# Layers 0 and 1 of a four-layer graph network: smaller parts of the orders' work, queued on VectorE behind the eviction of the sums they follow

## The chip, the cores and the metric

The kernel runs on one core of a Trainium2 chip, in fp32. The metric is the device time of one launch in microseconds (us), lower is better. TensorE does the matmuls and transposes, VectorE (DVE in the profile), ScalarE (ACT) and GpSimd (POOL) the elementwise work, SyncE (SP) issues most of the loads. [...] engines wait for each other at semaphores.

## The reference

Sixteen graphs of 1024 nodes with 256 features run through four layers, each of the form x = x + f(relu(layernorm(x)), adj). Layers 0 and 1 are one pass over the adjacency each; layer 2 updates the nodes one after the other, each from those before it; layer 3 is a sum and two dense layers.

```python
# layer 0
u = mask * jnp.exp(logits)                     # logits = e[:, :, None] + f[:, None, :] + a_b
a = u / jnp.sum(u, axis=2, keepdims=True)
h_prime = jnp.einsum('bnm,bmd->bnd', a, h)
# layer 1
d_inv_sqrt = (jnp.sum(adj, axis=-1) + 1e-05) ** (-0.5)
adj_norm = d_inv_sqrt[..., :, None] * adj * d_inv_sqrt[..., None, :]
return jnp.einsum('bnm,bmo->bno', adj_norm, support) + bias
# layer 2: a scan over i = 0 .. n-1
x_par = jnp.einsum('bj,bjd->bd', row, h)       # row = norm_adjT[:, i]
iou = x @ W_ioux.T + b_ioux + x_par @ W_iouh.T + b_iouh
h_new = z * x_par + (1.0 - z) * hc
# layer 3
neighbor_sum = jnp.einsum('bnm,bmd->bnd', adjacency, x)
h = jax.nn.silu(_rmsnorm(h, rms_weight))
```

## The kernel before

Layers 0 and 1 are one function, `layers_0_1`; layers 2 and 3 follow, and the change doesn't touch them. Batches run in a software pipeline: iteration i does layer 0 of batch i and layer 1 of batch i-1.

`layer_0(b)` first multiplies the adjacency with the exponentials `gs` (L361, into `pd`), then makes the neighbour sums in four groups of eight 128x512 matmuls (L309, `sums`). There are two groups for each half of the nodes: ScalarE evicts the first of a half (L312), VectorE the second (L314). Then come the row sums (L371), the reciprocals (L373 to L375), and the dense product (L379), which VectorE adds to x (L380). `layer_1(b)` does the same sums from `h1`, a product (L410) with its eviction (L411), the statistics, and `h2` (L301). The sums have two PSUM buffers (`pa`), the products two (`pmm`).

Between the four groups of a sum the lists `between` and `slots` put other jobs: `reshape` (statistics and h1 for layer 1), `prepare(i + 1)` (statistics, `q` at L340, `f` at L342, the exponential `gs` at L347 on ScalarE, the scaling at L352) and, from iteration 9 on, `put_in_order` for two batches (one in the last two iterations). `put_in_order` puts blocks of the adjacency and of h2 in layer 2's order: it loads `ad` (L423, L424) and `ab` (L427), masks and scales `ad` on GpSimd (L435 to L440), builds the permutation `to` (L432), transposes on TensorE (L448, L461, L463), evicts by turns on ScalarE and VectorE (L450, L452, L468, L470), multiplies (L476, L482), and writes `heT_d`, `near_d`, `next_d` and `base_d` through GpSimd's queue (L454, L472, L473, L485).

The orders are layer 2's plan, made from the zeros of the diagonal blocks. `places()` is a greedy pass over 128 positions: five small VectorE operations for each (L135 to L140), with the adjacency loaded in eight pieces of 16 (`piece`, L113, into a tile named `ad`). Then 8 pairs of 128x2048 operations rank the positions (L149, L151), and a transpose gives `place`, which `put_in_order` needs. `rest()` inverts the order with 128 operations (L162), writes the tables for the gathers of layer 2 (L174 to L181), makes a chain pass with eight pieces again (L195, L196), and counts the extra rounds (L201 to L236). Both are generators: `slot` takes the next part of `places` in each of the four slots of an iteration, from the start; `between[1]` and `between[3]` take one of `rest` from iteration 9 (`ready`) on.

The queue of each engine isn't this program order. A scheduler walks the program with a priority in the order of the text, puts an instruction into its engine's queue as soon as, by its own estimates, the inputs and a free buffer are there, and so may move work that is ready past work that still waits. Nothing in the kernel before ties the orders to a place in VectorE's queue. The pool `big01` has one buffer of most names; `ad` is one, shared by the pieces of both passes, the 128x2048 tiles of the ranking and `put_in_order`.

Of the kernel before, what the change touches and what calls it, by code (L numbers as in the profile page):

```python
# [9 lines left out]
F32 = mybir.dt.float32  # L10
# [30 lines left out]
def gnn_stack(ctx: ExitStack, tc: tile.TileContext, a: dict, out: bass.AP):  # L41
# [65 lines left out]
    def orders(pool, psum):  # L107
# [18 lines left out]
        def places():  # L126
            nc.vector.memset(bins, TOP)
            nc.vector.tensor_scalar(open_, step[:, :S], -1.0, TOP - 1, op0=ALU.mult, op1=ALU.add)
            nc.vector.tensor_scalar(below, open_, 1.0, None, op0=ALU.add)
            nc.vector.memset(held, 0.0)  # L130
            for j0 in range(0, P, S):
                nz = piece(j0, ALU.is_equal, 2 * TOP)
                for j in range(j0, j0 + S):
                    mine = bins[:, j : j + 1]
                    nc.vector.scalar_tensor_tensor(fit, below, mine, open_, op0=ALU.is_le, op1=ALU.mult)  # L135
                    nc.vector.tensor_reduce(mine, fit, AX.X, ALU.max)
                    nc.vector.scalar_tensor_tensor(held, open_, mine, held, op0=ALU.is_equal, op1=ALU.add)
                    nc.vector.scalar_tensor_tensor(open_, held, float(S), open_, op0=ALU.is_lt, op1=ALU.mult)
                    if j + 1 < P:
                        nc.vector.scalar_tensor_tensor(bins[:, j + 1 :], nz[:, j - j0, j + 1 :], mine, bins[:, j + 1 :],  # L140
                                                       op0=ALU.add, op1=ALU.min)
                    if j % 8 == 7:
                        yield

            key = tile_("key")
            nc.vector.scalar_tensor_tensor(key, bins, -256.0, step, op0=ALU.mult, op1=ALU.add)
            for i in range(0, P, S):
                less = pool.tile([P, S, P], F32, name="ad")
                nc.vector.tensor_tensor(less, key[:, None].to_broadcast([P, S, P]),  # L149
                                        key[:, i : i + S][:, :, None].to_broadcast([P, S, P]), ALU.is_lt)  # L150
                nc.vector.tensor_reduce(pos[:, i : i + S], less, AX.X, ALU.add)  # L151
                yield
            pt = psum.tile([P, 512], F32, name="pt")
            nc.tensor.transpose(pt[:, :P], pos, ident)
            nc.vector.tensor_copy(place, pt[:, :P])
            yield

        def rest():

            node = tile_("key")  # L160
            for p in range(P):
                nc.vector.scalar_tensor_tensor(junk, pos, float(p), step, op0=ALU.is_equal, op1=ALU.mult,  # L162
                                               accum_out=node[:, p : p + 1])
                if p % 32 == 31:
                    yield
# [17 lines left out]
            yield  # L183

            sub = tile_("sub")
            nc.vector.memset(sub, 0.0)
# [4 lines left out]
            for j0 in range(0, P, S):  # L191
                nz = piece(j0, ALU.not_equal, 2.0)
                for j in range(j0, min(j0 + S, P - 1)):
# [3 lines left out]
                                                   op0=ALU.mult, op1=ALU.max)  # L197
                yield
            top = tile_("top", NS)
            for s in range(NS):  # L200
                nc.vector.scalar_tensor_tensor(junk, sub, float(s), chain, op0=ALU.is_equal, op1=ALU.mult)  # L201
                nc.vector.tensor_reduce(top[:, s : s + 1], junk, AX.X, ALU.max)
# [34 lines left out]
            yield  # L237
        return places(), rest()

# [7 lines left out]
    def layers_0_1():  # L247
        with ExitStack() as st:
# [46 lines left out]
            def normed(x, scale, mv, name, bufs):  # L295
# [6 lines left out]
                return h  # L302

            def sums(at, h, ag):

                def part(n0, c):
# [6 lines left out]
                    else:  # L313
                        nc.vector.tensor_copy(ag[:, c, n0 : n0 + 512], pa)  # L314
                return [lambda n0=n0, c=c: part(n0, c) for n0 in (0, 512) for c in range(DC)]
# [39 lines left out]
            def layer_0(b, between):  # L355
# [9 lines left out]
                for part in sums(at[b], q[b], ag):  # L365
                    part()
                    if between:
                        between.pop(0)()
# [32 lines left out]
            def layer_1(b, between):  # L401
                ag = big.tile([P, DC, N], F32, name="ag", bufs=2)
                for part in sums(at[b], h1[b], ag):
                    part()
                    if between:
                        between.pop(0)()
# [85 lines left out]
            when.update({b + 2: (b,) for b in range(14, B)})  # L492
            parts_of_places, parts_of_rest = orders(big, psum)
            load(0)
# [3 lines left out]
            for i in range(B + 2):  # L498
                if i + 1 < B:
                    load(i + 1)  # L500
                jobs = []
                for b in when.get(i, ()):
# [12 lines left out]
                def slot():  # L515
                    for part in slots.pop(0):
                        part()
                    next(parts_of_places, None)
                if i < B:
# [6 lines left out]
                if 0 < i < B - 1:  # L526
# [3 lines left out]
                    between[1] = lambda: (load_half(i + 1), second())  # L530
                if i >= ready:
                    between += [lambda: None] * (4 - len(between))
                    for k in (1, 3):
                        between[k] = lambda part=between[k]: (part(), next(parts_of_rest, None))
                if 1 <= i <= B:
# [734 lines left out]
```

## Time and profile before

| | us |
|---|---|
| median of 3 runs | 4856.29 (4855.62 to 4856.56) |
| the profiled execution | 4861.04 |
| its span | 4858.2 |
| TensorE busy | 4494.9 |
| VectorE busy | 2303.1 |
| GpSimd busy | 1586.6 |
| ScalarE busy | 1220.2 |
| layers 0 and 1: first matmul of layer 2 | 1507.7 |

The profile is of one execution. Durations of one instruction are means of it unless a start is named; a group of one line can count records, not instructions (an fp32 matmul leaves two). "Idle before, releaser" tells what ended the idle time of an engine. A share of busy time is an average over stages with different limits, so the stage of layers 0 and 1, the first 31% of the span, has to be read by itself.

### The profile page before, as it was taken

To read this page: it belongs to the slowest core of one execution; us is meant where nothing else is said; L and a number is where in the kernel's file an instruction comes from. 1 tells how busy PE (TensorE), PEld (TensorE's weight loads), DVE (VectorE), ACT (ScalarE), POOL (GpSimd) and SP (SyncE) were. 2 spreads that over 40 slices of the span, in tenths; PEclk is the share of its full clock that TensorE was granted. 3 is DMA by queue.
4 is the path that set the end of the run, shared out by engine and by line. 5 is a ranking of instruction groups with operands and counts; after the bars stand their busy time and mean duration, and the time that the engine had idled before them with its cause. 6 is when DMAs were issued, how large, how long until landed. Compare 5 with 4: busy or idle time off the path is not lost. (4 is left out here: it accounts for less than half of the span.)

```text
span 4858.2 us, 52472 instructions
## 1 busy us (share of the span) xinstructions
PE 4494.9 (93%) x18199; PEld 3004.6 (62%) x18199; DVE 2303.1 (47%) x6354; ACT 1220.2 (25%) x2629; POOL 1586.6 (33%) x1939
## 2 busy tenths in 40 slices
PE   8998899999997999999999999998899999999999
PEld 4443455555555777777777777776455555555556
DVE  6667854455543444444444444454534344344342
ACT  1211112222212222222322222222223223223232
POOL 3223233343323322332232323331534234243231
PEclk9999999999998999999999999998899999999999
DMA  4333235555537444444344544420422231222100
GB/s 157 113 99 104 88 88 183 194 165 176 184 104 209 149 137 133 149 142 149 115 140 122 157 139 153 142 82 29 169 87 70 78 104 65 91 88 78 70 26 18
DMA packets 530978, 576.61 MB, mean 119 GB/s; under 512 B 42544, under 2 KB 439472, under 8 KB 528304
## 3 DMA queue, kind: packets, MB, share of 16 engines
q1 hardware_dynamic: 499536, 460.27, 30.6%
q0 software_dynamic: 31040, 111.44, 6.4%
q8 instruction: 197, 3.23, 0.3%
q14 instruction: 205, 1.68, 0.1%
HBM read 469.65 MB, written 116.65 MB: 121 GB/s over the span
## 5 line engine op out<-in xcount | busy, mean ns | idle before, releaser
L309 PE MATMUL pa<-at,h 128*128 128x512 f32 x1088 | 497.4, 610 | 32.9 <-DVE ag L314 32.9
L1145 PE MATMUL ph<-ag,w 128*128 128x512 f32 x1024 | 478.3, 609 | 32.7 <-DVE hh L1149 32.4
L1183 PE MATMUL po<-w,hh 128*128 128x256 f32 x2048 | 447.7, 379 | 0.0
L637 PE MATMUL pf<-hb,ab 128*128 128x256 f32 x1568 | 420.6, 387 | 29.0 <-DVE bxt L787 16.2
L1183 PEld LDWEIGHTS po<-w,hh 128*128 128x128 f32 x2048 | 387.8, 190 | 59.3 <-issue 7.9
L309 PE MATMUL pa<-at,q 128*128 128x512 f32 x960 | 424.2, 595 | 0.0
L309 PEld LDWEIGHTS pa<-at,h 128*128 128x128 f32 x1088 | 209.9, 196 | 278.5 <-issue 232.8
L749 PE MATMUL pf<-hs,wx 128*128 128x256 f32 x1536 | 351.1, 383 | 16.6 <-POOL hs L740 14.9
L1145 PEld LDWEIGHTS ph<-ag,w 128*128 128x128 f32 x1024 | 178.6, 189 | 294.0 <-DVE hh L1149 151.4
L1151 POOL TENSOR_TENSOR ss<-ss,sq 128x512 f32<-128x512 f32 x224 | 304.9, 1361 | 118.7 <-ACT sq L1148 114.3
L749 PEld LDWEIGHTS pf<-hs,wx 128*128 128x128 f32 x1536 | 292.1, 192 | 60.1 <-POOL hs L740 16.8
L637 PEld LDWEIGHTS pf<-hb,ab 128*128 128x128 f32 x1568 | 278.2, 192 | 69.5 <-DVE bxt L787 23.4
L309 PEld LDWEIGHTS pa<-at,q 128*128 128x128 f32 x960 | 178.2, 190 | 216.1 <-issue 212.6
L1149 DVE TENSOR_SCALAR hh<-ph,b 128x512 f32<-128x512 f32 x256 | 189.8, 746 | 153.8 <-ACT sq L1148 120.5
L784 PE MATMUL pf<-bd,h 128*128 128x384 f32 (+5 forms) x768 | 214.4, 373 | 51.7 <-DVE bxt L787 26.5
L1034 POOL DMA_INDIRECT hs_d<-h,table x128 | 129.3, 1010 | 365.4 <-ACT gates L757 179.7
L1130 PE MATMUL pa<-bxt,h 128*128 128x512 f32 x512 | 227.9, 597 | 18.6 <-POOL bxt L1112 18.6
L1130 PE MATMUL pa<-at,h 128*128 128x512 f32 x512 | 228.8, 597 | 0.0
L1148 ACT ACTIVATE sq<-ph,b 128x512 f32<-128x512 f32 x224 | 153.6, 686 | 233.6 <-PE ph L1145 188.2
L787 DVE TENSOR_TENSOR bxt<-bxt,pf 128x384 f32<-128x384 f32 (+5 forms) x384 | 141.2, 384 | 149.1 <-PE pf L784 146.6
L1175 ACT ACTIVATE hh<-hh,rw 128x512 f32<-128x512 f32 x256 | 168.4, 712 | 138.5 <-DVE hh L1174 136.5
L754 DVE TENSOR_TENSOR gates<-pf,bias 128x512 f32<-128x512 f32 x128 | 88.4, 691 | 227.3 <-PE pf L749 227.3
(253 smaller groups left out, 7318.6 us busy)
## 6 DMA issues: line engine op xcount, KB each, us to landing
at<-in_adjT SPq DMA_DIRECT2D x64, 1024.0 KB, 7.2
ab<-in_adj SPq DMA_DIRECT2D x128, 512.0 KB, 4.0
bxt<-in_adjT SPq DMA_DIRECT2D x64, 512.0 KB, 5.8
at<-in_adjT SPq DMA_DIRECT2D x64, 512.0 KB, 5.8
ad<-in_adj SPq DMA_DIRECT2D x128, 128.0 KB, 6.0
x_d<-x POOLq DMA_DIRECT2D x16, 1024.0 KB, 5.4
he_d<-h POOLq DMA_DIRECT2D x16, 1024.0 KB, 9.5
heT_d<-hT POOLq DMA_DIRECT2D x16, 1024.0 KB, 4.4
```

Of the source, the lines that this page charges most:

```text
L309: nc.tensor.matmul(pa, h[:, mt, c * P : (c + 1) * P], at[n0 // 512][:, mt], start=mt == 0, stop=mt == NT - 1)
L637: nc.tensor.matmul(pb, ab[:, jts[k]], hb[:, jts[k]], start=k == 0, stop=k == len(jts) - 1)
L749: nc.tensor.matmul(pg[:, e], wx[:, c, q * D + e * P : q * D + (e + 1) * P], self.hs[:, c], start=c == 0, stop=c == DC - 1)
L784: nc.tensor.matmul(pf, h[:, g, c * P : (c + 1) * P], bd[:, g, b4 : b4 + 4, S : S + far], start=True, stop=True)
L787: return lambda: nc.vector.tensor_add(to, to, pf)
L1130: nc.tensor.matmul(pa, h[b][:, mt, c * P : (c + 1) * P], at[b][n0 // NH][:, mt], start=mt == 0, stop=mt == NT - 1)
L1145: nc.tensor.matmul(ph, w1[:, c, k * P : (k + 1) * P], ag[:, c, n0 : n0 + NH], start=c == 0, stop=c == DC - 1)
L1148: nc.scalar.activation(sq, ph, AF.Square, bias=b1[:, k : k + 1])
L1149: nc.vector.tensor_scalar(hh[:, k], ph, b1[:, k : k + 1], None, op0=ALU.add)
L1151: nc.gpsimd.tensor_tensor(ss, ss, sq, ALU.add)
L1175: nc.scalar.activation(hh[:, k], hh[:, k], AF.Silu, scale=rw[:, k : k + 1])
L1183: nc.tensor.matmul(po, hh[:, c, k * P : (k + 1) * P], w2[:, c], start=c == 0, stop=c == HC - 1)
```

## The change

The orders' generators are cut into smaller parts, in three instead of two, and moved. A part of `places` is three positions instead of eight, or eight rows of the ranking instead of sixteen (the tile is half as large); a part of the new `tables` is eight of the L162 instead of 32; the chain pass, in the new `rounds`, yields after every eighth position instead of every sixteenth. The scratch `junk` of `rounds` is a tile of the name `ad` now.

`sums` keeps VectorE's evictions in the list `taken`, and `some_of(parts)` runs one part under `tc.issue_after(taken[-1].ins)`: each instruction that the part puts on VectorE's queue stands behind that eviction there. Instructions on other engines, its loads among them, aren't tied. `some_of` follows each of the four groups of a sum: in layer 0 with `places` before batch 9 and `tables` from there, in layer 1 with `places` and from batch 8 on `rounds`. What is left of `places` at iteration 9 runs at its start. The earlier calls in `slot` and `between` are gone.

```diff
-                    if j % 8 == 7:
+                    if j % 3 == 2:
                         yield
 
             key = tile_("key")
             nc.vector.scalar_tensor_tensor(key, bins, -256.0, step, op0=ALU.mult, op1=ALU.add)
-            for i in range(0, P, S):
-                less = pool.tile([P, S, P], F32, name="ad")
-                nc.vector.tensor_tensor(less, key[:, None].to_broadcast([P, S, P]),
-                                        key[:, i : i + S][:, :, None].to_broadcast([P, S, P]), ALU.is_lt)
-                nc.vector.tensor_reduce(pos[:, i : i + S], less, AX.X, ALU.add)
+            yield
+            for i in range(0, P, 8):
+                less = pool.tile([P, 8, P], F32, name="ad")
+                nc.vector.tensor_tensor(less, key[:, None].to_broadcast([P, 8, P]),
+                                        key[:, i : i + 8][:, :, None].to_broadcast([P, 8, P]), ALU.is_lt)
+                nc.vector.tensor_reduce(pos[:, i : i + 8], less, AX.X, ALU.add)
                 yield
...
-        def rest():
+        def tables():
...
-                if p % 32 == 31:
+                if p % 8 == 7:
                     yield
...
             yield
 
+        def rounds():
+
             sub = tile_("sub")
...
-                yield
+                    if j % 8 == 7:
+                        yield
             top = tile_("top", NS)
+            junk = pool.tile([P, P], F32, name="ad")
...
-        return places(), rest()
+        return places(), tables(), rounds()
...
+            taken = []
+
+            def some_of(parts):
+
+                with tc.issue_after(taken[-1].ins):
+                    next(parts, None)
+
             def sums(at, h, ag):
...
-                        nc.vector.tensor_copy(ag[:, c, n0 : n0 + 512], pa)
+                        taken.append(nc.vector.tensor_copy(ag[:, c, n0 : n0 + 512], pa))
...
                 for part in sums(at[b], q[b], ag):
                     part()
+                    if taken:
+                        some_of(places if b < ready else tables)
                     if between:
                         between.pop(0)()
...
                 for part in sums(at[b], h1[b], ag):
                     part()
+                    some_of(places if b + 1 < ready else rounds)
                     if between:
                         between.pop(0)()
...
+                if i == ready:
+                    for _ in places:
+                        pass
...
                     for part in slots.pop(0):
                         part()
-                    next(parts_of_places, None)
...
-                if i >= ready:
-                    between += [lambda: None] * (4 - len(between))
-                    for k in (1, 3):
-                        between[k] = lambda part=between[k]: (part(), next(parts_of_rest, None))
```

More of the change, by code (lines that the diff above doesn't have):

```diff
@@ L492, in layers_0_1 @@
             when.update({b + 2: (b,) for b in range(14, B)})
-            parts_of_places, parts_of_rest = orders(big, psum)
+            places, tables, rounds = orders(big, psum)
             load(0)
```

## The prediction

> **What bounds the kernel now.** I read the page first, then the clock and busy times stage by stage, then who TensorE waited for in the stage that the change touches, then the timelines of TensorE and VectorE around the longest wait.
>
> ```profile
> PE 4494.9 (93%) x18199; PEld 3004.6 (62%) x18199; DVE 2303.1 (47%) x6354; ACT 1220.2 (25%) x2629; POOL 1586.6 (33%) x1939
> ...
> 120.00:735.00 615.00, 556.03 (x1707) 281.82 (x1706) 417.88 (x1614) 108.50 (x227) 172.26 (x163) 0.96 0.33 98
> 735.00:1443.00 708.00, 673.08 (x2461) 382.34 (x2460) 360.51 (x1088) 143.65 (x288) 257.36 (x274) 0.98 0.53 173
> 1443.00:1508.00 65.00, 36.42 (x147) 26.50 (x146) 28.15 (x117) 9.57 (x18) 17.29 (x20) 0.73 0.50 164
> ```
>
> TensorE is the bound; the columns of the stretches are length, then busy time of PE, PEld, DVE, ACT, POOL, then the granted clock. Layers 0 and 1 fill 0 to 1508 us. Before 735 us TensorE is idle for 59 of 615 us, in the middle for 35 of 708, and in the last 65 us for 28, with the clock at 0.73. Who ends the idle time:
>
> ```profile
> PE pa L309 <- DVE ag L314: 32.9, 12, 4.9
> PE pd L361 <- ACT gs L347: 25.3, 2, 17.4
> PE pmm L410 <- DVE x L411: 14.5, 5, 5.3
> PE pt L461 <- ACT hT L468: 12.6, 7, 3.5
> PE pf L749 <- POOL hs L740: 11.5, 1, 11.5
> ```
>
> The columns are total, times, longest. The first and third are evictions late on VectorE. The second looks like ScalarE, but VectorE is behind it, as the two timelines at 452 to 488 us show (start, length):
>
> ```profile
> 455.14 2.28 DVE L149 TENSOR_TENSOR ad<-o_key 128x2048 f32<-128x2048 f32 x1
> 457.34 0.68 DVE L314 COPY ag<-pa 128x512 f32<-128x512 f32 x1
> ...
> 479.19 0.94 DVE L342 SCALAR_TENSOR_TENSOR junk<-q,rs,v 128x256 f32<-128x256 f32 x1
> ...
> 485.60 2.27 DVE L151 TENSOR_REDUCE o_pos<-ad 128x16 f32<-128x2048 f32 x1
> 487.79 0.67 DVE L314 COPY ag<-pa 128x512 f32<-128x512 f32 x1
> ...
> 458.07 8.83 PE L309 MATMUL pa<-at,h 128*128 128x512 f32 x16 [2.97 <-DVE ag L314]
> 466.74 1.89 PE L410 MATMUL pmm<-w,ag 128*128 128x256 f32 x8
> 486.07 5.55 PE L361 MATMUL pd<-at,gs 128*32 128x512 f32 x26 [17.44 <-ACT gs L347]
> ```
>
> Between 455 and 490 us twelve 2.28 us operations of the orders (L149, L151) alternate with the eight L342 that make f; the exponential of L347 needs all eight, and L361 needs the exponential. The eviction L314 is 30 us after its predecessor.
>
> [...] the copy at 457.34 starts as L149 ends, though its sum was complete. [...] here 0.96 and 0.73 stand beside the stalls, against 1.00 in 600 to 800 us, where no gap passes 1.5. [...] L342 takes 0.47 or 0.94 us. [...]
>
> **The change part by part.** In the built programs each engine holds the same instructions before and after, but for 16 more on VectorE: L149 and L151 become 16 pairs of half size. No instruction of layers 2 and 3 moves on any engine. [...] All else is order.
>
> *How much may stand ahead of an eviction.* One sum group (8 matmuls, 16 records) takes 6.93 us (27.73 for four in the timeline), so the two L314 of a sum come 13.86 us apart. In layer 1 the first is always late: its VectorE chain (statistics, q, f) ends just in time. From its end TensorE has 6.93 us of sums and 1.73 of L410 before it needs the second L314 and one L411 (0.69 + 0.48): 7.5 us are left for orders. The observed cases fit: 48 operations of places and one L114 took 9.9 us and the stall at 383.8 was 2.49; the stall after 43 of L162 (14.6 us) was 5.31.
>
> *Before 735 us.* (a) The first L314 of layer 1 cost 23.8 us in eight stalls (3.72, 3.39, 4.89, 1.43, 2.97, 4.54, 1.44, 1.44). Two batches without orders in that gap still show 1.44, with some 22 us of work there; at 26 to 28 us of work it is 3 to 5, about half a us per us, since part fills VectorE's own waits. In the new order these gaps hold 23, 26, 27, 26, 25, 26, 26, 22 us (instruction counts times durations less 0.08 of overlap): 3.7+3.0+3.6+3.4+2.6+2.6+2.6+1.4 = 23. Gain 1. (b) L410 behind the second L314 cost 3.69+1.36+2.49+5.31 = 12.9. The new gaps hold 63, 4, 50, 4, 48 operations of places (the first held 69)[...]: stalls of 2.8, 0, 1.4, 0, 2, 0, 0. Gain 6.6. (c) The wait of 17.4 goes: two half-size operations at most now stand among the f. (d) L379 waited 3.62+0.40+0.80 behind 45 of L162 and a conversion; the new gap has four half-size operations. Gain 4.8. Together 30 us. The clock of 0.96 over 615 us is 25 us of lost clock, some 7 of it while TensorE stood still anyway; [...] I take 7. **Gain 37.**
>
> *735 to 1443 us.* Work of the orders that ran early now comes later: the 128 L162 (0.32 us each with the accumulator read, 41 us) move from 510-580 us to batches 9 to 13, beside the chain pass (L195, L196), whose pieces share the single buffer `ad` with the loads of put_in_order. So put_in_order leaves its regular place in batches 10 to 14 and lands between L379 and L410, as it does before only in batches 13 to 15. There the trace shows 7.7 us of stalls for one such batch (at 1170 to 1195 us: 0.47, 4.30, 1.02, 1.86), against about 3 in a regular one. Four more such batches: 4 x 4.5 less what batches 14 and 15 save by becoming regular (6) = 12. The tables now come in batch 14: 16 issues of L177 (1.1 to 1.3 us apart on SP in the trace) stand before refills of `ad`, and on GpSimd two pairs of L181 (2.76 us each) wait for them in front of near_d, next_d and heT_d, whose landing frees hT. SP: about 9 us ahead of one refill, covered by some 12 us of matmuls. GpSimd: 5.5 + 2.4 landing, twice, of which I take half, 8 us, less the 0 of before. Bound: 0 if the matmuls cover all, 25 if none. [...] I take 19 in all, bounds -5 and 40. **Loss 19.**
>
> *The tail.* From the last layer 1 sum (1443) to the first matmul of layer 2 (1507.7) are 64.7 us; two put_in_order and the end of the orders (L201 to L236) are in it. In the new order the orders end two batches earlier and put_in_order(14) stands among the last sums. What remains: L410 7.0, last L411 and statistics 1.1, rs 2.4, h2 4.1, transposes and copies 3, heT_d issue and landing 4.8, the rest of ao with L476 and bo 9.3 (1487.0 to 1496.3), then 11.5 to layer 2: 43 us. Of the 21 us saved, put_in_order(14) costs 7 at full clock where it goes and the L222 2. **Gain 12.**
>
> Sum: -37 + 19 - 12 = -30 us on the profiled execution of 4861.0 (span 4858.2), which is 4.7 above the median of 4856.3. On the median: 4826 us.
>
> **The rivals.** *B, the middle costs nothing*: the irregular batches are hidden; for it, refills of `ad` had 5.1 us to landing and 12 us of cover. -37 - 12 = -49: 4807. *C, the stalls only move*: VectorE does the same work, and eight stalls of class (a) stay; if class (a) takes the full us per us (10 us more) and the middle costs its 40, -27 + 40 - 12: 4857, no change. *D, slower: the single buffer `ad`*. Each of the 16 put_in_order needs issue 0.43, landing 5.1, then select and two multiplications on GpSimd (1.2 + 2.0 + 1.75): 10.5 us, hidden so far. In batches 10 to 14 the pieces of the chain pass, the scratch of L201 to L214 and ten put_in_order take turns in it. Against 49 us of gain it decides from five uncovered refills on; seven give +24: 4880. Against it: the order leaves 12 us or more of matmuls between most users. That the parts don't go behind the sums is excluded by the built order.
>
> **How the numbers follow.** Main case 0.52 (4812 to 4838), B 0.24, C 0.14, D 0.10. The likeliest is 4826; the range 4798 to 4852 leaves out most of D and the far end of B. A difference under 0.2% (9.7 us) can't be told from none. Faster: 0.51 of the main case, 0.24, and 0.04 of C: 0.79. Slower: D and 0.01 of C: 0.11. Same: 0.10.
>
> **What would show it.** Right: no wait of L361 for L347 beyond 2 us in the middle; L410 <- L411 at half of 14.5 or less; L309 <- L314 still near 30; a clock above 0.97 before 735 us; the tail some 20 us shorter. The middle would show new waits of L448 and L461. Wrong: L114 or L435 waiting long for loads of `ad`, or waits of L309 for L314 that have grown by 10 us or more.

## The result and the profile after

The changed kernel takes 4880.1 us (median of six, 4869.7 to 4896.3) against 4856.4 for the kernel before (six, 4855.4 to 4864.2): a ratio of 1.0045 [1.0033, 1.0057]. It is slower by 0.45%, where 4826 was forecast. The profiled execution takes 4878.5 us, its span is 4876.5. These are its busy times:

```profile
PE 4509.6 (92%) x18199; PEld 3002.6 (62%) x18199; DVE 2294.9 (47%) x6370; ACT 1220.4 (25%) x2629; POOL 1578.5 (32%) x1939
```

The stretches of the prediction in the trace after (length, then busy time of PE, PEld, DVE, ACT, POOL, the granted clock, DMA share, GB/s). The last sum matmul now ends at 1489 us instead of 1443, so the tail is cut there:

```profile
120.00:735.00 615.00, 583.25 (x1821) 292.59 (x1820) 384.43 (x1400) 116.02 (x240) 158.26 (x163) 0.97 0.34 109
735.00:1443.00 708.00, 631.85 (x2256) 356.32 (x2255) 382.87 (x1363) 131.90 (x265) 263.16 (x271) 0.95 0.51 159
1489.00:1531.00 42.00, 21.02 (x80) 14.67 (x78) 13.01 (x37) 6.74 (x13) 7.10 (x10) 0.75 0.46 155
```

Ahead of 735 us TensorE is busy 583 us instead of 556: the early gain is there. In the middle it is busy 632 instead of 673, and its clock is 0.95 instead of 0.98: the loss is there, and it is larger than the gain. The tail is 42 us instead of 65. TensorE's waits from 0 to 1530 us (total, times, longest):

```profile
PE pa L321 <- DVE ag L326: 32.6, 11, 4.9
PE pt L476 <- ACT hT L483: 23.3, 4, 15.9
PE pt L463 <- ACT hT L465: 20.4, 4, 9.5
PE pt L476 <- POOL ad L454: 11.3, 3, 8.2
...
PE pd L373 <- ACT gs L359: 7.7, 1, 7.7
PE pmm L425 <- DVE x L426: 7.0, 4, 3.2
```

Line numbers are up to 15 higher than before, and those of each experiment are its own: L309, L314 are now L321, L326; L347, L361 are L359, L373; L410, L411 are L425, L426; L448 and L461 are L463 and L476; L181 is L182. The evictions of the sums cost the same as before (32.9), and the wait for the exponential that cost 17.4 is gone (the 7.7 is at the start). L425 for L426 is halved. Rows two to four, 55 us in all, have grown: put_in_order waits for the buffers hT and ad. In the kernel before the same three waits come to 18.3 us, the 12.6 of L461 for L468 in the prediction's table and these two:

```profile
PE pt L461 <- POOL ad L439: 4.1, 2, 3.1
...
PE pt L448 <- ACT hT L450: 1.6, 3, 0.9
```

Cut at the first L361 (L373) of each batch, the profiled executions compare so. The first row is the start of iteration 9, the last the first matmul of layer 2, the others lengths; the columns to the right are experiments, told below. All in us:

| | before | after | table_sync | ds_after | after_bias | early_tables | ds_early | ds_early_bias | no_rounds |
|---|---|---|---|---|---|---|---|---|---|
| start of 9 | 741.3 | 711.1 | 711.0 | 710.7 | 710.8 | 723.6 | 724.3 | 727.5 | 724.8 |
| 9 | 94.5 | 94.7 | 95.1 | 99.1 | 92.5 | 93.8 | 94.0 | 84.1 | 92.7 |
| 10 | 92.3 | 102.0 | 101.9 | 100.8 | 102.8 | 101.9 | 102.8 | 107.8 | 92.0 |
| 11 | 93.8 | 102.3 | 101.8 | 108.8 | 99.7 | 101.1 | 105.2 | 96.4 | 92.4 |
| 12 | 97.9 | 117.3 | 117.7 | 110.7 | 94.0 | 96.0 | 102.5 | 95.3 | 94.5 |
| 13 | 99.0 | 80.6 | 80.6 | 124.3 | 92.6 | 93.0 | 103.8 | 96.9 | 93.7 |
| 14 | 97.3 | 155.9 | 136.1 | 92.7 | 137.7 | 125.4 | 91.5 | 89.6 | 94.7 |
| 15 and tail | 191.6 | 167.3 | 167.6 | 168.2 | 168.2 | 171.1 | 167.1 | 169.2 | 167.0 |
| layer 2 | 1507.7 | 1531.3 | 1511.7 | 1515.2 | 1498.3 | 1506.0 | 1491.3 | 1466.9 | 1451.7 |

The change gains 30.2 us up to iteration 9, loses 19.4 from there to the end of iteration 13 and 34.3 behind it (156 us in iteration 14, less 24 in the rest). Sum: +23.6 at the first matmul of layer 2. Iteration 14, GpSimd's timeline in the trace after (start, length, operation, and in brackets the idle time before it with what ended it):

```profile
1224.07 2.84 POOL L182 DMA_DIRECT2D table<-order_d  x1
1233.54 2.75 POOL L182 DMA_DIRECT2D table<-order_d  x1 [6.63 <-issue]
...
1238.09 0.97 POOL L488 DMA_DIRECT2D next_d<-hT  x1
...
1253.02 2.79 POOL L182 DMA_DIRECT2D table<-order_d  x1 [0.91 <-DMA order_d<-o_sub]
1265.31 2.75 POOL L182 DMA_DIRECT2D table<-order_d  x1 [9.49 <-issue]
1268.05 0.57 POOL L469 DMA_DIRECT2D heT_d<-hT  x1
...
1277.64 0.11 POOL L472 MEMSET hT<- 128x16 f32 x1 [8.12 <-DMA heT_d<-hT]
```

And TensorE beside it, then ScalarE, whose copies it waits for:

```profile
1251.71 1.97 PE L463 MATMUL pt<-to,h 128*128 128x128 f32 x8 [9.48 <-ACT hT L465]
...
1278.33 0.47 PE L476 MATMUL pt<-to,ad 128*128 128x128 f32 x1 [15.94 <-ACT hT L483]
...
1251.08 1.07 ACT L465 COPY hT<-pt 128x512 f32<-128x512 f32 x2 [7.28 <-DMA next_d<-hT]
...
1277.69 0.58 ACT L483 COPY hT<-pt 128x512 f32<-128x512 f32 x1 [22.60 <-DMA heT_d<-hT]
```

Each pair of table loads keeps GpSimd's queue for 12 and 15 us, of which 6.6 and 9.5 are "issue", in which nothing that the profile shows is waited for. The times of landing tell more: the load of 1253.02 landed at 1264.92, and the one behind it starts at 1265.31. So it is in the kernel before (landed 601.71, next 602.15; landed 621.27, next 621.61): the second load of a pair starts when the first has landed. What makes it wait is not in the trace. next_d stands behind the first pair and heT_d behind the second, and heT_d, issued at 1268.05 right behind the last load, lands only after some 9.6 us. Both read hT, so ScalarE can't write the next hT until they have landed, and TensorE waits 9.48 and 15.94 us. Beside and behind these waits its granted clock was 0.50 from 1252 to 1256 and from 1268 to 1280 us, and 0.69 in the mean of 1246 to 1284, by an estimate 12 us of lost clock (0.31 x 38). The DMA view of 1200 to 1290 us compares the loads with heT_d (KB each, median us from issue to landing):

```profile
heT_d<-hT POOLq DMA_DIRECT2D x2, 1024.0 KB, 4.2
...
table<-order_d POOLq DMA_DIRECT2D x4, 32.0 KB, 10.5
```

32 KB of table take 10.5 us and a megabyte of heT_d 4.2. The table's elements, of 4 bytes each, are gathered across order_d; in the trace a load is 128 packets of 256 bytes. Why it takes longer than the megabyte is not shown.

### The profile page after: what moved, and what is told of

It is laid out like the page before. It is cut to its first block, busy times and chain, and to the rows that moved or that the text cites. A ratio compares the mean times of both kernels' runs of the same rounds, so it can differ in the third digit from the quotient of the medians.

```text
span 4876.5 us, 52487 instructions
## 1 busy us (share of the span) xinstructions
PE 4509.6 (92%) x18199; PEld 3002.6 (62%) x18199; DVE 2294.9 (47%) x6370; ACT 1220.4 (25%) x2629; POOL 1578.5 (32%) x1939
## 5 line engine op out<-in xcount | busy, mean ns | idle before, releaser
L321 PE MATMUL pa<-at,h 128*128 128x512 f32 x1088 | 503.6, 614 | 32.6 <-DVE ag L326 32.6
L321 PE MATMUL pa<-at,q 128*128 128x512 f32 x960 | 426.6, 597 | 0.0
L321 PEld LDWEIGHTS pa<-at,h 128*128 128x128 f32 x1088 | 211.2, 197 | 275.4 <-issue 230.7
L762 PE MATMUL pf<-hs,wx 128*128 128x256 f32 x1536 | 350.8, 383 | 18.3 <-POOL hs L753 16.4
L321 PEld LDWEIGHTS pa<-at,q 128*128 128x128 f32 x960 | 179.5, 191 | 220.8 <-issue 218.1
```

What stands on the lines that cost most here:

```text
L321: nc.tensor.matmul(pa, h[:, mt, c * P : (c + 1) * P], at[n0 // 512][:, mt], start=mt == 0, stop=mt == NT - 1)
L762: nc.tensor.matmul(pg[:, e], wx[:, c, q * D + e * P : q * D + (e + 1) * P], self.hs[:, c], start=c == 0, stop=c == DC - 1)
```

## The experiments

Ratios are to runs of the kernel before on the same chip, whose median was 4857 to 4861 us in the five groups of runs. The names are those used in the table above.

| | median us | ratio to before |
|---|---|---|
| places_new | 4872.0 | 1.0026 [1.0017, 1.0034] |
| rest_new | 4888.7 | 1.0056 [1.0037, 1.0074] |
| in_turn | 4877.0 | 1.0033 [1.0020, 1.0046] |
| table_sync | 4864.5 | 1.0011 [1.0003, 1.0019] |
| loads_twice | 4874.5 | 1.0024 [1.0014, 1.0034] |
| early_tables | 4859.8 | 0.9998 [0.9990, 1.0006] |
| turn_sync | 4865.0 | 1.0010 [1.0002, 1.0018] |
| no_pins | 4889.6 | 1.0063 [1.0050, 1.0076] |
| early_old_rounds | 4868.7 | 1.0010 [1.0000, 1.0020] |
| early4_old_rounds | 4895.1 | 1.0063 [1.0043, 1.0082] |
| early_pinned_rounds | 4869.6 | 1.0018 [1.0009, 1.0026] |
| own_junk | 4874.2 | 1.0021 [1.0014, 1.0029] |
| ds_after | 4857.6 | 1.0002 [0.9993, 1.0010] |
| ds_early | 4844.6 | 0.9968 [0.9956, 0.9980] |
| ds_early3 | 4860.5 | 0.9999 [0.9989, 1.0009] |
| after_bias | 4851.0 | 0.9987 [0.9976, 0.9997] |
| ds_early_bias | 4814.5 | 0.9916 [0.9902, 0.9930] |

### The halves of the change

places_new keeps the change in places alone; rest_new keeps it in tables and rounds alone.

```diff
 # places_new, in layer_0 (layer_1 likewise); rest() and its places between[1], between[3] as before
-                    if taken:
-                        some_of(places if b < ready else tables)
+                    if taken and b < ready:
+                        some_of(places)
```

> Only places has the small parts and the issue behind the sums; the tables and the rounds are as in the kernel before (parts of 32, two per iteration, not pinned). Theory 1 (the whole loss is in how tables and rounds are queued): the early gain of 27 us stays, middle and tail as before: 4829, 4822 to 4838, first matmul of layer 2 near 1481. Rival (the parts pinned behind the sums cost in themselves, and the early gain is given back when the work that waited is done): 4850 or more, with new waits between 735 and 1443 us.

> The other half: places as before (parts of 8 and 16, not pinned), tables and rounds as in the changed kernel. Theory 1: no early gain, the middle's loss of 72 less the tail's 22 stays: 4856 + 50 = 4906, 4893 to 4918, with the idle times of 9.5 and 15.9 us before L463 and L476 in it. Rival (gain and loss are one: VectorE that ran ahead early is late in the middle): 4885 or less.

places_new misses its forecast by 43 us: 4872. Its iteration 9 starts at 726.7 us, and iterations 8 and 9 take 95.1 and 121.6 us, 43 more than the 79.3 and 94.7 of the changed kernel. That is where the table loads stand in it (721 to 761 us), now that places ends later and the first put_in_order has begun. So a loss is there also with tables cut and queued as before, and it stands where the table loads stand.

rest_new gives 4889 where 4906 was expected and 4885 or less by the rival, because it too has an early gain, though places is as before and the wait of 17.4 us for the exponential is still in it: its iteration 9 starts at 719.4 us, 21.9 earlier than before. The 128 L162, at 505 to 578 us in the kernel before, now run from 717 us on, and iteration 6 alone takes 84.4 us instead of 102.1. So a large part of the early gain comes from where this work went and not from the smaller parts of places. Where it runs early again (515 to 595 us in no_pins, 510 to 643 in early_tables, both below), 15.8 and 17.7 us of the 30.2 are left.

### The table loads

in_turn lets layer 1's places take table parts before the rounds; table_sync puts the four loads on SP's queue; turn_sync does both.

```diff
 # in_turn, layer_1; rest goes through tables, then rounds
-                    some_of(places if b + 1 < ready else rounds)
+                    some_of(places if b + 1 < ready else rest)
 # table_sync
-                        nc.gpsimd.dma_start(table[k][:, g].rearrange("p t s -> p (t s)"),
+                        nc.sync.dma_start(table[k][:, g].rearrange("p t s -> p (t s)"),
```

> The changed kernel, with the rounds begun only when the tables are through (layer 1's places take table parts first). The tables' DMAs come some 150 us earlier and their buffer o_sub has not been used by the rounds. Theory 1 (tables' DMAs stand in GpSimd's queue in front of next_d and heT_d, whose landing frees hT): the waits of 9.5 and 15.9 us go, with half-clock time of some 12 us: 4880 - 35 = 4845, 4835 to 4856; the four table DMAs may cost a part of it at their new place. Rival (put_in_order thrown out of its place by the shared buffer ad costs the middle): 4868 to 4890.

> The changed kernel with the four table loads on SP's queue and none on GpSimd's. Theory 1: near_d, next_d and heT_d go out without the four loads of 2.8 us and the 6.6 and 9.5 us that they waited: 4845 to 4860, PE's waits of 9.5 and 15.9 us below 4 each. Rival a: the same 25 us come back on SP, whose loads for the next put_in_order then stand behind: 4875 to 4890. Rival b (the middle's loss is elsewhere): 4870 to 4885 with those two waits gone.

> Tables before rounds, as in in_turn (4877), with the four table loads on SP's queue. Theory 1b: iteration 11, 133 us in in_turn against 93 in before, comes down to 100 to 110: 4877 - 27 = 4850, 4842 to 4862. Rival (the loss there is the irregular put_in_order, not the loads): 4868 or more.

in_turn only moves the loss: iteration 14 is mended, and iteration 11, in which the loads now stand, takes 133.0 us. table_sync brings iteration 14 from 155.9 to 136.1 us and the ratio from 1.0045 to 1.0011. The waits of 9.48 and 15.94 us become 2.4 and 2.1, and 5.2 and 2.6 follow them. turn_sync saves only 10 us in its iteration 11 (123.2, where 100 to 110 was expected), the rest having moved to SP's queue, where the loads that follow a table load are late in their turn (a wait of 8.1 us for h<-he_d). So rival a of table_sync is partly right too.

loads_twice measures the loads by themselves: the kernel before, in which they are made once more.

```diff
 -                nc.gpsimd.dma_start(next_d[b].rearrange("t j n -> j t n"), ao[:, : NT - 1, P + S :])
+                sent = nc.gpsimd.dma_start(next_d[b].rearrange("t j n -> j t n"), ao[:, : NT - 1, P + S :])
+                if b in (6, 7):
+                    k = b - 6
+                    with tc.issue_after(sent.ins), nc.allow_non_contiguous_dma(reason="indices, once"):
+                        for g in range(G2):
+                            nc.gpsimd.dma_start(table[k][:, g].rearrange("p t s -> p (t s)"),
+                                                order_d[k].rearrange("t s b i -> (b i) (t s)")[g * GR : (g + 1) * GR])
```

> The kernel before, in which the four table loads are made once more from order_d (the same values), two behind next_d of batch 6 and two behind next_d of batch 7 in GpSimd's queue, where put_in_order is under way. No VectorE work is added. Theory 1b (the loads hold GpSimd's queue, 14 us for each pair, and heT_d and the select of ad stand behind them): 4860 + 33 = 4893, 4880 to 4905, with waits of L448 and L461 of 8 us and more in that iteration. Rival (the tables cost by their VectorE part, L162, and by the writes of order_d): within 8 us of before.

It costs 14 us, and iteration 12 is 13.4 us longer, so the loads alone cost something, but less than half of what was expected. TensorE's waits from 1020 to 1140 us, and GpSimd's last pair:

```profile
PE pt L461 <- ACT hT L468: 10.4, 2, 7.4
```

```profile
1082.90 2.79 POOL L478 DMA_DIRECT2D table<-order_d  x1
1096.09 2.76 POOL L478 DMA_DIRECT2D table<-order_d  x1 [10.41 <-issue]
```

The queue is held as long as in the changed kernel, but only by this pair: between the two loads of the first one (1052.55 and 1064.64 us) GpSimd does the masking of put_in_order. And order_d had been written long before. Where the loads come right behind the writes of order_d, an iteration is 32 to 39 us longer: 133.0 us in in_turn against 93.8 in before, and in early4_old_rounds (below), the cleanest case, 125.9 us in iteration 9 with the loads in it against 93.8 in early_old_rounds without them. How the difference from 14 us divides between the writes, GpSimd's wait for them and the work around them was not taken apart.

early_tables takes places in parts of five rows and goes on to the tables, so that the loads stand ahead of the first put_in_order:

```diff
-                    if j % 3 == 2:
+                    if j % 5 == 4:
 # first goes through places, then tables, in layer_0 and layer_1 up to iteration 9
-                        some_of(places if b < ready else tables)
+                        some_of(first)
```

> The changed kernel with places in parts of five rows instead of three, and the tables' parts next in the same row, so that the table loads come before the first put_in_order; rounds as in the changed kernel. Theory 1b: most of the early gain stays (22 to 30 us of it), the 39 us of the tables go, rounds between the put_in_order of iterations 9 to 13 cost their 19 and the tail gains 12 or more: 4860 - 26 + 19 - 12 = 4841, 4830 to 4854. Rival (larger parts fill the gaps that the change had emptied, and the tables cost before iteration 9 what they cost behind it): 4862 or more.

4860, equal to before. The loads, at 655 to 689 us, now cost nothing that can be seen (TensorE waits 2.6 us in all of iteration 8). But with the larger parts, and with the 128 L162 early again, 17.7 us of the early gain are left instead of 30.2; iterations 10 and 11 are as long as in the changed kernel, and 14 takes 125.4 us against 97.3 in the kernel before. There is a second loss.

### The pins and the rounds

> The changed kernel with its small parts at the same places, but none queued behind the sums: the scheduler puts their instructions where it likes. The 128 L162 go early again, the table loads stay late on GpSimd. Theory 1b: iteration 14 with its 156 us stays, and of the early gain of 27 us perhaps half, by the small parts alone: 4880 to 4900. Rival (the pins throw put_in_order out of its place, and that is the loss): 4862 or less.

Without the pins (some_of calls only next) it takes 4890, and iteration 14 still 155.5 us: the pins are no part of the loss. The early gain falls to half, as expected (iteration 9 starts at 725.5); the ratios, 1.0063 and 1.0045 with the pins, lie too close to say how much of that the whole time keeps.

early_old_rounds is early_tables with the rounds of before (16 rows, two per iteration, not pinned); early_pinned_rounds pins those; early4_old_rounds has places in parts of four rows. In all three the scratch of the rounds stays in ad, as in the changed kernel.

> early_tables (4860), with the rounds as in the kernel before: parts of 16 rows, two per iteration, not pinned. Theory 2 (beside the table loads it is the rounds, in four pinned parts of 8 rows per iteration, that push put_in_order from its place and cost the 16 us of iterations 9 to 14): the early gain of 18 us is left: 4860 - 18 = 4842, 4834 to 4851, first matmul of layer 2 near 1490. Rival (whatever was not done before iteration 9 is paid for later, by any order): 4854 to 4864.

> As early_old_rounds (rounds in parts of 16 rows, two per iteration), but each part queued behind the sums. Theory 2a (the pin costs): 4853 to 4865, like early_tables. Theory 2b (the size and the number of the parts cost, not the pin): within 5 us of early_old_rounds.

> As early_old_rounds, with places in parts of four rows instead of five, so that the tables end in iteration 8 to 9. Theory 1b and 2: 5 us more of the early gain if the table loads are still ahead of the first put_in_order: 4838, 4830 to 4848. Rival (the loads now meet the first put_in_order, as in places_new): 4850 to 4872, with a wait of 7 us or more before L463 or L476 in iteration 9.

Theory 2 falls: 4869 and 4870, no better than early_tables, pinned or not, large parts or small. early4_old_rounds fell on its rival's side, further than the rival said: the tables end one iteration too late, the loads meet the first put_in_order, and a stall of 14.1 us stands in iteration 9. Its waits there:

```profile
PE pt L475 <- ACT hT L482: 14.1, 1, 14.1
PE pt L462 <- ACT hT L464: 4.2, 1, 4.2
```

no_rounds leaves the rounds out and sets the numbers of extra rounds to zero:

```diff
         def rounds():
-            sub = tile_("sub")
...
             for k in range(2):
...
+                nc.vector.memset(more[k], 0)
             yield
```

> early_tables without rounds: more is set to zero, so the extra rounds of layer 2 and 3 are not done and only the time to the first matmul of layer 2 is to be read. If the rounds are the second loss: iterations 9 to 14 take 92 to 95 us each, as 9 to 11 do in the kernel before, and layer 2 begins at 1475 or earlier (early_tables: 1506). If put_in_order is out of its place for another reason: iterations 10, 11 and 14 still take 101, 101 and 125.

Iterations 9 to 14 take 92 to 95 us (one execution) and layer 2 begins at 1451.7, 54.3 us earlier than in early_tables. So the second loss is with the rounds, through a buffer or through VectorE. The 54.3 us don't measure it: the kernel before makes the rounds too, and here none are made.

### The buffer ad

own_junk puts only the scratch of the end of rounds back into o_junk. ds_after moves the pieces too, into ds, which is free while layer 1 sums. ds_early is the same on early_tables. ds_early3 has parts of three rows again, but 16 columns to a comparison and 16 of the L162 to a part.

```diff
 # ds_after, ds_early, ds_early3
-            for j0 in range(0, P, S):
-                nz = piece(j0, ALU.not_equal, 2.0)
+            for j0 in range(0, P, 8):
+                nz = pool.tile([P, 8, P], F32, name="ds")
+                for t in range(NT):
+                    nc.sync.dma_start(nz[t * B : (t + 1) * B], a["adj"][:, t * P + j0 : t * P + j0 + 8, t * P : (t + 1) * P])
...
-            junk = pool.tile([P, P], F32, name="ad")
```

> The changed kernel, with the scratch of the end of rounds (L202 to L219) in its own tile o_junk, as in the kernel before, and not in ad. If the single buffer ad sets the end of rounds (rival D of the prediction): 4865 to 4875, the waits of L476 for ad shorter. If the loads and the parts do: 4876 to 4886.

> The changed kernel with the rounds' pieces, eight rows each, in the buffer ds (free from the end of layer 0's sums to the next iteration) and their scratch in o_junk, so that only put_in_order uses ad. If the single ad is the second loss (rival D of the prediction): 4880 - 12 for the scratch - 16 = 4852, 4844 to 4862; the table loads still cost their part. If it is VectorE's work: 4866 to 4876 (own_junk 4874).

> early_tables with the same pieces in ds and scratch in o_junk. If ad is the second loss: 4860 - 20 = 4840, 4830 to 4850. If VectorE's work is: 4852 to 4862.

> ds_early, with places in parts of three rows as in the changed kernel, its comparisons in eight parts of 16 columns and the tables in parts of 16, so that the table loads still precede put_in_order. Early gain of 27 us instead of 18: 8 us less than ds_early. Rival (the twelve 2.28 us operations of L149 and L151, though pinned, delay f and L361 again): as ds_early or 5 us more.

The scratch alone is worth 12 us (1.0045 to 1.0021, iteration 14 from 155.9 to 143.6), scratch and pieces 21 (1.0002). The waits of L476 for ad, which the forecast for own_junk named, stayed as they were (11.3 and 11.0 us); what fell is the longest wait of L476 for hT, from 15.9 to 6.2 us, and in the changed kernel that one stood behind the second pair of table loads. So in iteration 14 the scratch and the loads act together. On early_tables, where the loads are out of the way, scratch and pieces are worth 15 us (0.9998 to 0.9968): ds_early is 4845, the first kernel that beats the one before. ds_early3, 16 us slower than ds_early, fits neither of its forecasts; it loses its gain before iteration 9, which starts at 736.7 (iteration 8 takes 100.0 us). But in ds_early iterations 10 to 13 take 103 to 105 us, so the buffer was not all.

### VectorE beside GpSimd

In early_tables three views of 974 to 989 us stand together. VectorE:

```profile
974.74 9.79 DVE L352 TENSOR_SCALAR q<-x,mv 128x256 f32<-128x256 f32 x1
984.45 0.17 DVE L296 BATCH_NORM_AGGREGATE mv<-s 128x2 f32<-128x6 f32 x1
984.54 0.32 DVE L352 TENSOR_SCALAR q<-x,mv 128x256 f32<-128x256 f32 x1
...
987.64 0.68 DVE L485 COPY hT<-pt 128x512 f32<-128x512 f32 x1
```

GpSimd:

```profile
974.29 1.10 POOL L450 TENSOR_SCALAR_AFFINE_SELECT ad<-ad 128x1024 f32<-128x1024 f32 x1
975.35 1.69 POOL L455 TENSOR_TENSOR ad<-ad,dinv 128x896 f32<-128x896 f32 x1
976.99 1.90 POOL L454 TENSOR_TENSOR ad<-ad,dinv 128x1024 f32<-128x1024 f32 x1
978.82 0.11 POOL L472 MEMSET hT<- 128x16 f32 x1
978.89 5.48 POOL L413 TENSOR_TENSOR x<-x,bias_sb 128x256 f32<-128x256 f32 x8
```

And TensorE:

```profile
988.37 0.47 PE L476 MATMUL pt<-to,ad 128*128 128x128 f32 x1 [7.04 <-DVE hT L485]
```

One L352, 0.32 us when nothing is beside it, takes 9.79, as long as GpSimd runs without a pause, over twelve of its instructions; it ends 0.2 us after the last of them. The eviction L485 stands behind it and TensorE waits 7.04 us. Here GpSimd's additions of the bias (L413) had piled up and ran in one go. From iteration 9 on the kernel before has, beside a `to` of 2.57 us (L432), one operation held over 2.2 us (L79, 3.31); the changed one has L352 with 3.82 and L426 with 4.81 among others, ds_early one L356 with 5.71. In the regular case the starts of the two engines' operations alternate; VectorE's timeline of the changed kernel at 1071 us, and GpSimd's:

```profile
1070.60 0.80 DVE L352 TENSOR_SCALAR q<-x,mv 128x256 f32<-128x256 f32 x1
1071.32 0.94 DVE L354 SCALAR_TENSOR_TENSOR junk<-q,rs,v 128x256 f32<-128x256 f32 x1
```

```profile
1071.21 0.77 POOL L413 TENSOR_TENSOR x<-x,bias_sb 128x256 f32<-128x256 f32 x1
1071.94 0.90 POOL L357 TENSOR_TENSOR x<-x,W_b_sb 128x256 f32<-128x256 f32 x1
```

L352 and L354 then take 0.80 and 0.94 us. While GpSimd has nothing to do, 0.32 is seen for the one (early_tables, 984.54) and 0.48 for the other (L356 of ds_early, 993.85). The L352 of 974.74 in early_tables got no such turn: its time covers all twelve of GpSimd's instructions. What decides between the two engines is not in the traces.

Most of this isn't new with the change. Summed over VectorE's instructions from the start of iteration 9 to layer 2, the time above the usual length of the same instruction (an estimate; usual is what the shortest twentieth of its kind takes in these traces) is 69 us in the kernel before and 90 in the changed one.

after_bias and ds_early_bias move these additions to VectorE in the last batches:

```diff
-                    nc.gpsimd.tensor_tensor(x[b][:, t], x[b][:, t], vec["W_b"], ALU.add)
+                    (nc.gpsimd if b <= ready else nc.vector).tensor_tensor(x[b][:, t], x[b][:, t], vec["W_b"], ALU.add)
...
-                    nc.gpsimd.tensor_tensor(x[b][:, t], x[b][:, t], vec["bias"], ALU.add)
+                    (nc.gpsimd if b < ready else nc.vector).tensor_tensor(x[b][:, t], x[b][:, t], vec["bias"], ALU.add)
```

> The changed kernel with the same bias additions on VectorE. If GpSimd's runs hold VectorE: 4880 - 12 = 4868, 4858 to 4873; the table loads and the single ad still cost theirs. If VectorE's amount of work is the loss: 4880 to 4895.

> ds_early with the bias additions L359 (from batch 10 on) and L415 (from batch 9 on) on VectorE instead of GpSimd, 16 operations per iteration, some 7 us more of VectorE. If GpSimd's back-to-back runs hold VectorE: the operations of 4 to 6 us are gone but for those beside the select and multiplications of ad, iterations 10 to 13 go from 103 to 105 to 95 to 99, and the time from 4845 to 4822, 4815 to 4832. If VectorE's amount of work is the loss: 4845 to 4858, since there is more of it.

VectorE has more to do and the kernel gets faster: ds_early from 4845 to 4814 (0.9916), the changed kernel from 4880 to 4851 (0.9987), 28 us by the ratios, more than twice what was expected there. No operation but `to` (L449, 2.69) is held over 2.2 us in ds_early_bias. That VectorE's amount of work was the loss is excluded.

What the move frees is two things, though. The time above the usual length, estimated as before, falls from 90 to 39 us in after_bias and from 76 to 39 in ds_early_bias. But GpSimd's queue gets shorter too, and ds_early shows that this counts. GpSimd, VectorE and TensorE there:

```profile
984.99 1.66 POOL L83 TENSOR_TENSOR rs<-rs_v,mhalf 128x8 f32<-128x8 f32 x1
986.63 5.47 POOL L359 TENSOR_TENSOR x<-x,W_b_sb 128x256 f32<-128x256 f32 x8
...
986.68 5.71 DVE L356 SCALAR_TENSOR_TENSOR junk<-q,rs,v 128x256 f32<-128x256 f32 x1 [8.32 <-POOL rs L83]
...
992.32 1.28 DVE L469 COPY hT<-pt 128x512 f32<-128x512 f32 x2
...
993.10 0.45 PE L478 MATMUL pt<-to,ad 128*128 128x128 f32 x1 [11.05 <-POOL x L359]
```

VectorE first stands idle for 8.32 us: rs, whose input was there at 972.8, stands in GpSimd's queue behind the masking of ad and six additions of the bias. Only then does L356 start, and it takes 5.71 us beside the run of eight (0.48 at 993.85). TensorE's 11.05 us have both in them. VectorE's waits for rs before this operation fall from 22.9 us in ds_early to 5.8 in ds_early_bias. How the gain divides between the holding and the shorter queue isn't settled; no run takes the additions off GpSimd without giving them to VectorE.

ds_early_bias's iterations 11 to 13 come to 95 to 97 us as expected, and iteration 10 does not (107.8). Its middle and its longest waits for put_in_order, in the stretch of 735 to 1443 us and from 735 to 1500:

```profile
735.00:1443.00 708.00, 677.33 (x2511) 390.22 (x2509) 383.20 (x1293) 146.32 (x295) 191.66 (x181) 0.98 0.53 175
```

```profile
PE pt L465 <- DVE to L449: 7.8, 3, 3.6
PE pt L478 <- ACT hT L485: 7.2, 5, 4.2
```

TensorE is busy 677 us of the 708, with VectorE as busy as in the changed kernel (383) and GpSimd at 192 instead of 263. ds_early_bias is the best version. The same move was not tried in the kernel before, where the alternating pairs are slow as well (L342: median 0.94 us, shortest 0.47); so the 28 us are more likely a bound on what the change lost here than a measure of it.

## Why the prediction was wrong

**Early, "Gain 37": right, a little too large.** 30.2 us by the start of iteration 9. Idle time ahead of 735 us fell from 59.0 to 31.8. Point (a), eight stalls of the first L314, was to go from 23.8 to 23 and came to 28.2. Point (b) came from 12.9 to 3.6 (6.2 predicted), (c) and (d) went to nothing as predicted. What is left for the clock is about 3 us (30.2 less 27.2); the 7 taken for it was the author's estimate. The ranking's half-size operations (1024 wide; L150, L152) take 1.21 us where the full ones took 2.28, so its 16 pairs cost 2.4 us of VectorE more than the 8 of before. Where the gain comes from was seen in part only: rest_new gets 21.9 us with the wait of point (c) still in it, where of the work ahead of iteration 9 only that of the tables, the L162 above all, has moved.

**The tail, "Gain 12": right.** What is left of it is 42.7 us against 43 forecast, and put_in_order(14) did move into the middle.

**The middle, "Loss 19", bounds -5 to 40: this is the step that failed.** The stage begins 30.2 us earlier and the last sum ends 45.4 us later, so the middle lost 75.6 us. Some 9 of them are work that was to move here from the tail; 67 stand against the 19. (The term's own parts, 12 and 8, make 20 already.) Three things in it were wrong.

- The tables, put at 8 us with a bound of 25. The mechanism was named rightly (L181 on GpSimd in front of near_d, next_d and heT_d), but a pair was taken as 5.5 us of issue and 2.4 of landing. It holds the queue 12 to 16 us: the second load started only 0.3 to 0.5 us after the first had landed. The trace before had this at the loads' own line, L181, as idle time of GpSimd and as time to landing (the 2.4 is the median there for order_d, L177):

```profile
  issue: 20.7, 3
DMA to landing us min/median/max: 9.0/9.1/10.0
```

But there the loads stood in iteration 7, where nothing waited. Moving them to SP gives back 16 us, and an iteration is 32 to 39 us longer where they follow the writes of order_d at once.
- The single buffer ad, part of the 12 for irregular batches and the main thing of rival D, which had a chance of 0.10. It costs 21 us in the changed kernel, 12 by the scratch that the change itself put there and the rest by the pieces, and 15 where the loads are out of the way. D's total, 4880, is the measured one by luck: its mechanism makes up less than a third of the 67.
- GpSimd's work that piles up was in no sum. The prediction saw L342 at 0.47 or 0.94 and put no price on it. As far as the timelines show, GpSimd's operations ran in one go once put_in_order had left its place: single VectorE operations of the changed kernel are held for up to 5 us (9.79 in early_tables), with the evictions behind them, and what VectorE needs from GpSimd stands in its queue. Moving the additions away gives back 28 us; how much of that the change had cost is open.

One by one the three give back 65 us by their ratios. ds_early_bias, which has all three mended (the loads by being early), takes 739.4 us from the start of iteration 9 to layer 2, the changed kernel 820.2 and the kernel before 766.4: together they mend the loss and 27 us more. How they share it is not settled.

Of the signs for being right, nearly all came: the wait of L361 is gone, L410 for L411 is halved, L309 for L314 is near 30, the tail is 22 us shorter, and the clock before 735 us is 0.97, though not above it. They watch the early part and the tail, where the prediction was right. The sign for the middle, waits of L448 and L461 (L463 and L476), came too, without a size by which to judge it. The sign for being wrong, long waits of L114 or L435 for loads of ad, did not come: GpSimd's L435 waits 49.2 us for these loads in the kernel before and 19.6 in the changed one (L450), L114 not at all, and L309 for L314 has not grown. Rival C was right that the stalls of class (a) stay, and its 40 for the middle was still too little. That the stalls only move is not what the runs show: ds_early has gained 17.0 us at the start of iteration 9 and 16.4 at layer 2.

## What to carry to other kernels

Before work is moved to another stage, ask which of its instructions hold a queue: a gather of 4-byte elements held GpSimd's for 12 to 16 us per pair, free of charge while nothing stood behind it, and with an iteration up to 39 us longer where something did. The time from issue to landing (9 to 13 us) says more of it than the length of the issue (2.8). An engine's spare share says nothing of such queues, nor of an operation that lasts as long as another engine's run (9.79 us instead of 0.32): look for single operations that take many times their usual length, and for what the other engine runs in that time. Moving 16 small additions per iteration from GpSimd to the busier VectorE gained 25 to 28 us by the ratios, more than any single change of order here; whether the kernel before would gain as much was not tried. And see where work goes that you move: a large part of the early gain was the 128 L162 leaving the stage.

## What the hardware showed

A VectorE operation of 128x256 took 9.79 us instead of 0.32 beside a run of twelve GpSimd operations and ended 0.2 us after the last of them (early_tables); where the two engines' operations alternate it took 0.80 (changed kernel, 1070.60). TensorE's granted clock was 0.50 from 1268 to 1280 us of the changed kernel, beside its wait of 15.94 us. A DMA of 32 KB, gathered from elements of 4 bytes (128 packets of 256 bytes in the trace), landed after 9 to 13 us (9.0 to 10.0 in the kernel before, 9.9 to 11.9 in the changed one, 12.8 the longest in loads_twice). On GpSimd's queue the load behind it started 0.3 to 0.5 us after that landing, with 5.0 to 10.4 us of idle time before it; a heT_d behind the last load was issued at once and landed after some 9.6 us, against a median of 4.2. On SP's queue two such loads took 10.28 us to issue, and another DMA behind one of them 4.9 to 7.3 us (turn_sync).
